# A mixture of 64 experts on one core: three sequences of the first layer are sorted by expert and run in units of 128 rows

## The chip, the core and the metric

The kernel runs on one NeuronCore of a Trainium2 chip. The metric is device time in microseconds for one execution. All arithmetic is float32.

## What is computed

The input `x` has 8 sequences of 512 tokens with 128 features. Three layers follow each other, each on a layer norm of the running sum: half of a mixture-of-experts block, a small mixing block along the sequence, and half of the same mixture-of-experts block again.

```python
def ffn(x):                      # xf: 4096 tokens x 128
    shared = silu(xf @ Ws_up) @ Ws_down            # 128 -> 64 -> 128
    aff = xf @ centroids.T                         # 64 experts
    _, idx = top_k(aff + expert_biases, 8)
    w = sigmoid(take_along_axis(aff, idx, axis=1))
    w = w / (sum(w, -1, keepdims=True) + 1e-8)
    cw = zeros((T, 64)).at[arange(T)[:, None], idx].add(w)
    h = silu(einsum('td,edf->etf', xf, W_up))      # 128 -> 64, every expert
    y = einsum('etf,efd->etd', h, W_down)          # 64 -> 128
    return shared + einsum('etd,te->td', y, cw)
x = x + 0.5 * ffn(layernorm(x))
x = x + mixing(layernorm(x))     # two 128x128 products, one gate per token
x = x + 0.5 * ffn(layernorm(x))
```

Each token uses 8 of the 64 experts; the weight of the other 56 in `cw` is zero. The reference computes all 64 and so does the kernel before.

## The kernel before, in words

An *item* is one sequence in one mixture-of-experts layer: 16 items, layer 0 first (`items`, L293). Within an item the experts go in 32 *pairs*. One step of the main loop (L478 on) is one pair of one item, 512 steps in all. In step n:

- `up(n)` (L419): one product of 128 x 128 weights (two experts side by side, `wup`) with 512 tokens (`ut`, tokens along the free side) into a bank of `ps_up`, then the silu on ScalarE into a tile `h` of the pool `hid`.
- `scale(n - SCALE_LAG)` (L428): VectorE multiplies `h` with the routing weights `cw` of the pair. These lie in SBUF repeated over the 64 rows of each expert. `load_cw` (L299) fetches them for GROUP pairs at a time, by two broadcasting transfers issued on SP, from `cw_t` in DRAM; after the last pair of a group has been scaled, `scale` calls `load_cw` for the group CW_BUFS further on.
- `down(n - DOWN_LAG)` (L437): one product of `wdn` with the scaled `h`, summed over all 32 pairs in a bank of `ps_y`. In between, the shared expert's product (L456) is added to the same bank.
- one step of `prep(i + 1)`, a generator: layer norm (`stats`, L181, with two small operations on GpSimd), turning, the shared expert's up and the affinities (L334), and the routing: eighth largest, weights, turned (`pc`, L387) and written to `cw_t`. In layer 1 the mixing block (`mix`, L219) comes first. Two steps after the last down of an item, `finish` adds the result to `x` (L409) and in layer 1 writes it out.

Every engine works its instructions in the order in which the program issues them: the schedule is written out by hand (`manual_schedule`). All DMAs are issued on SP. SCALE_LAG is 22, DOWN_LAG 25, GROUP 4, CW_BUFS 4. The start is set apart: the weights and two sequences are loaded ahead (L125 to L137); at step FIRST (14) of the first item its `prep` is run to its end, CW_BUFS groups are asked for, and then `load_rest` (L139) issues the rest of the down weights, the other six sequences and small constants, before any further group.

PSUM has eight banks: four for `ps_up`, two for `ps_y`, two for everything else (`ps_m`).

Of the kernel before, what the change touches and what calls it, by code (L numbers as in the profile page):

```python
# [8 lines left out]
F32 = mybir.dt.float32  # L9
AF = mybir.ActivationFunctionType  # L10
# [7 lines left out]
GROUP = 4  # L18
SCALE_LAG = 22
DOWN_LAG = 25  # L20
CW_BUFS = 4
FIRST = 14
SHARED = (8, 16)
# [3 lines left out]
def macaron_kernel(  # L27
# [33 lines left out]

    nc = tc.nc
# [5 lines left out]
    D1 = D + 1  # L68
    H = T // 2
# [9 lines left out]
    hid = ctx.enter_context(tc.tile_pool(name="hid", bufs=DOWN_LAG + 3))  # L79
    dram = ctx.enter_context(tc.tile_pool(name="dram", bufs=2, space=bass.MemoryType.DRAM))  # L80
    ps_up = ctx.enter_context(tc.tile_pool(name="ps_up", bufs=4, space=bass.MemoryType.PSUM))
    ps_y = ctx.enter_context(tc.tile_pool(name="ps_y", bufs=2, space=bass.MemoryType.PSUM))
    ps_m = ctx.enter_context(tc.tile_pool(name="ps_m", bufs=2, space=bass.MemoryType.PSUM))
# [17 lines left out]
    wup = const.tile([P, E, F], F32, name="wup")  # L101
    wdn = const.tile([P, NP, D], F32, name="wdn")
# [11 lines left out]
    def load_up(e0, e1):  # L114
        nc.sync.dma_start(
            out=wup[:, e0:e1, :], in_=w_up[e0:e1].rearrange("e d f -> d e f")
        )

# [20 lines left out]
    def load_rest():  # L139
# [4 lines left out]
        for s in range(2, B):  # L144
            load_x(s)
# [7 lines left out]
        nc.sync.dma_start(out=b_bc, in_=b.partition_broadcast(P))  # L153

    def transposed(dst, src, rows):
        ps = ps_m.tile([P, 512], F32, tag="m", name="turn_ps")
# [3 lines left out]
    turn_ps = ps_m.tile([P, 512], F32, tag="m", name="cent_ps")  # L160
# [8 lines left out]
    def make_mix():  # L169
        for k, (dst, src) in enumerate(((mix_b, wb_sb), (mix_bf, wbf_sb))):  # L170
            transposed(dst[:, :D], src, D)
            ps = ps_m.tile([P, 512], F32, tag="m", name="gate_ps")
# [5 lines left out]
        nc.scalar.mul(half_b, b_bc, 0.5)  # L178

# [17 lines left out]
    def normed(src, mv, rstd, width, name):  # L197
        u = norm.tile([P, NT, width], F32, tag=f"u{width}", name=f"u_{name}")
# [11 lines left out]
    def turned(dst, src, name, parts=1):  # L210

        for part in range(parts):
            js = range(part * NT // parts, (part + 1) * NT // parts)
            ps = ps_m.tile([P, len(js) * P], F32, tag="m", name=f"ps_{name}_{part}")
# [4 lines left out]
    def mix(s):  # L219
# [3 lines left out]
        u = normed(xt, mv, rstd, D1, f"mix{s}")  # L223

        for k, j in ((0, 0), (1, NT - 1)):
            ew = norm.tile([P, D], F32, tag="ew", name=f"ew{s}_{k}")
# [6 lines left out]
        ut = norm.tile([P, T + 1], F32, tag="mixt", name=f"mixt{s}")  # L233
# [5 lines left out]
        gam = small.tile([P, NT], F32, tag="gam", name=f"gam{s}")  # L239
        halves = []  # L240
        for half in range(NT // 2):
            pfb = ps_m.tile([P, 2, D1], F32, tag="m", name=f"pfb{s}_{half}")
            halves.append(pfb)
            for k in range(2):
# [20 lines left out]
            nc.scalar.activation(  # L265
                gam[:, 2 * half : 2 * half + 2],
                pfb[:, :, D],
                AF.Tanh,
                bias=half_b,
                scale=0.5,  # L270
            )
            yield
        sg = small.tile([P, NT], F32, tag="sg", name=f"sg{s}")
        nc.vector.tensor_scalar(sg, gam, 0.5, 0.5, ALU.mult, ALU.add)
        rest = small.tile([P, NT], F32, tag="rest", name=f"rest{s}")
        nc.vector.tensor_scalar(rest, gam, -0.5, 0.5, ALU.mult, ALU.add)
        for j in range(NT):
            nc.vector.scalar_tensor_tensor(
                xt[:, j, :],
                halves[j // 2][:, j % 2, :D],  # L280
                sg[:, j : j + 1],
                xt[:, j, :],
                ALU.mult,
                ALU.add,
            )
        yield
        for j in range(NT):
            nc.vector.scalar_tensor_tensor(
                xt[:, j, :], u[:, j, :D], rest[:, j : j + 1], xt[:, j, :], ALU.mult, ALU.add
            )  # L290
        yield

    items = [(layer, s) for layer in range(2) for s in range(B)]  # L293
    uts = {}
    shared = {}
    cw_ts = {}
    cw_tiles = {}

    def load_cw(g):  # L299

# [202 lines left out]
    for k in sorted(later):  # L503
        later[k]()
# [40 lines left out]
```

## Time and profile before

| what | value |
|---|---|
| median of 3 runs | 963.33 us (963.13 to 963.34) |
| the profiled execution itself | 963.14 us |
| its span, first to last instruction | 961.4 us |
| instructions | 8274 |
| TensorE clock granted | 1.000 |
| moved by DMA | 145.71 MB, mean 152 GB/s |

How to read it. The page gives the busy time of each engine (PE is TensorE, DVE is VectorE, ACT is ScalarE, POOL is GpSimd, SP the engine that issues the DMAs), the same in 40 slices of 24 us as tenths, the chain of work that ended last, and groups of instructions: line, engine, operation, output and inputs, shapes, count, then busy time and mean duration of one, and the idle time ahead of them with what ended it. A float32 product appears as two MATMUL instructions and two weight loads, a transpose as one. The ends of matmuls are modelled and overlap, so their cadence is read from the starts in the timeline.

### The profile page before, as it was taken

How to read it: one execution, taken by the hardware profiler on the slowest of the kernel's cores; microseconds unless marked ns; L12 is line 12 of the kernel's file. 1: busy time of each engine (PE TensorE's matmuls, PEld its weight loads, DVE VectorE, ACT ScalarE, POOL GpSimd, SP SyncE). 2: the span in 40 equal slices, each digit the busy share in tenths (PEclk: the TensorE clock that was granted, in tenths of full speed). 3: DMA queues.
4: the chain of work that ended last, by engine and by line, in shares of the span. 5: the costliest groups of instructions: out<-in, count | busy, mean ns of one | idle time of the engine just before them, and what ended most of it. 6: DMA issues, size and time to landing. Idle time of an engine off the chain costs nothing.

```text
span 961.4 us, 8274 instructions
## 1 busy us (share of the span) xinstructions
PE 949.5 (99%) x2535; PEld 441.6 (46%) x2535; DVE 476.0 (50%) x1282; ACT 398.6 (41%) x674; POOL 39.8 (4%) x73
## 2 busy tenths in 40 slices
PE   7999999999999999999999999999999999999998
PEld 3444444444444444454444544445444454444443
DVE  3453463515536253455464554645546455466243
ACT  6643353434434343344353443533435334353330
POOL 1000000000000000000000000000000000000000
PEclk9999999999999999999999999999999999999999
DMA  7999868496874869737677476784767848678933
GB/s 175 220 214 215 173 133 163 104 180 132 169 163 98 164 141 183 149 88 169 124 174 158 88 180 124 171 171 88 176 126 172 171 88 173 126 173 182 209 73 81
DMA packets 90188, 145.71 MB, mean 152 GB/s; under 512 B 10080, under 2 KB 24096, under 8 KB 90144
## 3 DMA queue, kind: packets, MB, share of 16 engines
q1 hardware_dynamic: 90144, 145.18, 71.9%
q8 instruction: 20, 0.33, 0.2%
q14 instruction: 24, 0.20, 0.1%
HBM read 140.97 MB, written 4.19 MB: 151 GB/s over the span
## 4 chain that ended last, share of the span: by engine, by line
PE 98%; ACT 1%; DVE 1%; DMA 0%; POOL 0%; issue 0%; ACTq 0%
PE y L441 46%; PE ph L423 45%; PE sl L334 2%; PE y L456 1%; PE po L407 1%; PE ps_ft L216 1%; PE pfb L253 1%; PE pfb L246 1%; PE pa L350 0%; PE ps_mixt L216 0%; PE pc L387 0%; ACT L425 0%; DMA x<-in_L_attn_u_dram 0%; ACT h L425 0%; DVE lg L343 0%; POOL rstd_f L194 0%
## 5 line engine op out<-in xcount | busy, mean ns | idle before, releaser
L423 PE MATMUL ph<-ut,wup 128*128 128x512 f32 x1024 | 522.7, 595 | 1.7 <-ACT h L425 1.7
L441 PE MATMUL y<-h,wdn 128*128 128x512 f32 x1024 | 519.0, 592 | 0.0
L425 ACT ACTIVATE h<-ph 128x512 f32<-128x512 f32 x512 | 303.3, 597 | 443.6 <-PE ph L423 414.6
L431 DVE TENSOR_TENSOR h<-h,cw 128x512 f32<-128x512 f32 x512 | 322.1, 682 | 51.7 <-DMA cw<-cw_t 49.2
L441 PEld LDWEIGHTS y<-h,wdn 128*128 128x128 f32 x1024 | 194.8, 190 | 244.6 <-issue 210.9
L423 PEld LDWEIGHTS ph<-ut,wup 128*128 128x128 f32 x1024 | 186.8, 191 | 196.0 <-issue 190.2
L409 DVE TENSOR_TENSOR x<-po,x 128x512 f32<-128x512 f32 (+1 forms) x17 | 11.2, 660 | 180.5 <-PE po L407 180.4
L343 DVE COPY lg<-sl 64x256 f32<-64x256 f32 x32 | 13.5, 422 | 99.5 <-PE sl L334 92.4
L262 DVE SCALAR_TENSOR_TENSOR pfb<-u_mix,ident,pfb 128x129 f32<-128x129 f32 x16 | 5.7, 356 | 93.8 <-PE pfb L253 80.1
L193 POOL TENSOR_SCALAR rstd_f<-mv_f 128x4 f32<-128x4 f32 (+1 forms) x17 | 8.7, 511 | 506.1 <-DVE mv_f L191 506.1
L200 DVE TENSOR_SCALAR u_f<-x,mv_f,rstd_f 128x128 f32<-128x128 f32 x64 | 17.9, 342 | 19.7 <-POOL rstd_f L194 19.7
L344 ACT ACTIVATE hsh<-sl 64x256 f32<-64x256 f32 x32 | 12.1, 378 | 32.6 <-DVE lg L343 32.6
L425 ACT ACT_TABLE_LOAD x16 | 20.5, 1283 | 0.3
L361 ACT ACT_TABLE_LOAD x16 | 20.5, 1283 | 0.3
L189 DVE BATCH_NORM_STATS2 st_f<-x 128x6 f32<-128x128 f32 x64 | 13.9, 277 | 12.7 <-DMA x<-in_L_attn_u_dram 12.7
L334 PE MATMUL sl<-ut,wsl 128*128 128x256 f32 x64 | 17.4, 397 | 0.0
L194 POOL TENSOR_TENSOR rstd_f<-rstd_f,minus_half 128x4 f32<-128x4 f32 (+1 forms) x17 | 16.8, 991 | 1.4
L193 POOL TENSOR_SCALAR rstd_mix<-mv_mix 128x4 f32<-128x4 f32 x8 | 4.6, 575 | 293.4 <-DVE mv_mix L191 293.4
L334 PEld LDWEIGHTS sl<-ut,wsl 128*128 128x128 f32 x64 | 12.4, 199 | 8.5 <-issue 6.7
L265 ACT ACTIVATE gam<-pfb,half_b 128x2 f32<-128x2 f32 x16 | 4.2, 262 | 25.2 <-DVE pfb L262 25.2
L325 ACT COPY ut<-ps_ft 128x512 f32<-128x512 f32 (+1 forms) x17 | 9.5, 560 | 12.2 <-PE ps_ft L216 12.2
L246 PEld LDWEIGHTS pfb<-mix_b,mixt 128*128 128x128 f32 x64 | 10.9, 191 | 7.6 <-issue 5.7
(69 smaller groups left out, 280.3 us busy)
## 6 DMA issues: line engine op xcount, KB each, us to landing
cw<-cw_t SPq DMA_DIRECT2D x256, 512.0 KB, 7.2
cw_t<-cw_sb SPq DMA_DIRECT2D x32, 64.0 KB, 4.2
x<-in_L_attn_u_dram SPq DMA_DIRECT2D x7, 256.0 KB, 5.7
out_dram<-x SPq DMA_DIRECT2D x7, 256.0 KB, 2.3
wdn<-in_L_ffn_W_down_dram SPq DMA_DIRECT2D x2, 512.0 KB, 5.9
wup<-in_L_ffn_W_up_dram SPq DMA_DIRECT2D x2, 256.0 KB, 4.2
wup<-in_L_ffn_W_up_dram SPq DMA_DIRECT2D x1, 512.0 KB, 6.9
x<-in_L_attn_u_dram SPq DMA_DIRECT2D x2, 128.0 KB, 2.2
```

Of the source, the lines that this page charges most:

```text
L189: nc.vector.bn_stats(st[:, j, :], src[:, j, :])
L193: nc.gpsimd.tensor_scalar(rstd[:, at], mv[:, at, 1], EPS_LN, None, ALU.add)
L194: nc.gpsimd.tensor_tensor(rstd[:, at], rstd[:, at], minus_half[:, at], ALU.pow)
L200: nc.vector.tensor_scalar(u[:, j, :D], src[:, j, :], mv[:, j, 0:1], rstd[:, j : j + 1], ALU.subtract, ALU.mult,)
L246: nc.tensor.matmul(pfb[:, k, :], lhsT=ut[:, j * P : (j + 1) * P], rhs=mix_b, start=True, stop=False,)
L334: nc.tensor.matmul(sl[:, k, :], lhsT=wsl[:, k, :, :].rearrange("d a f -> d (a f)"), rhs=ut[:, k * H : (k + 1) * H], start=True, stop=True,)
L343: nc.vector.tensor_copy(lg[other, :], sl[other, k, :])
L361: nc.scalar.activation(sig, pa, AF.Sigmoid)
L423: nc.tensor.matmul(ph, lhsT=w, rhs=uts[i], start=True, stop=True)
L425: nc.scalar.activation(h, ph, AF.Silu)
L431: nc.vector.tensor_tensor(h, h, cw_tiles[group][:, g, :], ALU.mult)
L441: nc.tensor.matmul(ys[i], lhsT=wdn[:, pair, :], rhs=hs.pop(n), start=pair == 0 and i % 2 == 0, stop=pair == NP - 1,)
```

## The change

Three of the eight sequences of layer 0 (5, 6 and 7) leave the dense stream, which keeps 13 items. They are handled beside it, in the same loop, by `background`, called once at the end of each step:

1. `sorted_chunk` prepares the three sequences one after the other (layer norm, turning, affinities, routing; the shared expert is added at once), then counts, by products with triangular matrices of ones, at which place of a list sorted by expert each token's eight copies lie, and in which place of a list in which each expert begins on a multiple of 128 rows.
2. For each tile of 128 tokens and each of its 8 experts, GpSimd scatters 128 rows of 512 B to `xsort` in DRAM: 96 indirect DMAs, at most POOL_RATE (1.25) per step.
3. 160 units of 128 rows, in quads of four, one quad every 3 steps: SP reads four row numbers into registers and loads the rows; ScalarE reads four expert numbers into registers and copies that expert's weights from `wup` and from `wtwice` (the down weights once more, in both halves of the partitions) to fixed places; TensorE turns the rows and runs up and down for one expert per unit; SP stores the result in `ysort` in DRAM.
4. GpSimd gathers, for each tile and each of its 8 experts, 128 rows of `ysort`: 96 indirect DMAs, again 1.25 per step; VectorE adds each, times its weight, to `x`, ADD_LAG (4) steps after its issue.

The lags of the dense stream become 9 and 11, its weights come in 3 groups of 2 pairs, FIRST is 8; `ps_up` has two banks, `ps_un` (transposes, units, results) two, and `ps_m` one for each of two streams. `load_rest` loads the sorted sequences first and gains `load_twice`.

The core of the diff:

```diff
-GROUP = 4
-SCALE_LAG = 22
-DOWN_LAG = 25
-CW_BUFS = 4
-FIRST = 14
-SHARED = (8, 16)
+GROUP = 2
+SCALE_LAG = 9
+DOWN_LAG = 11
+CW_BUFS = 3
+FIRST = 8
+SHARED = (16, 24)
+HID_BUFS = DOWN_LAG + 2
+CHUNKS = [(0, (5, 6, 7))]
+DENSE = [(0, s) for s in range(5)] + [(1, s) for s in range(8)]
+LATER_X = (5, 6, 7, 2, 3, 4)
+QUAD = 4
+UNIT_LAG = 4
+UNIT_PERIOD = 3
+POOL_RATE = 1.25
+BACK_BUFS = 7
+ADD_LAG = 4
...
-    hid = ctx.enter_context(tc.tile_pool(name="hid", bufs=DOWN_LAG + 3))
+    hid = ctx.enter_context(tc.tile_pool(name="hid", bufs=HID_BUFS))
+    unit = ctx.enter_context(tc.tile_pool(name="unit", bufs=2))
+    chunk = ctx.enter_context(tc.tile_pool(name="chunk", bufs=1))
+    back = ctx.enter_context(tc.tile_pool(name="back", bufs=BACK_BUFS))
     dram = ctx.enter_context(tc.tile_pool(name="dram", bufs=2, space=bass.MemoryType.DRAM))
-    ps_up = ctx.enter_context(tc.tile_pool(name="ps_up", bufs=4, space=bass.MemoryType.PSUM))
+    ps_up = ctx.enter_context(tc.tile_pool(name="ps_up", bufs=2, space=bass.MemoryType.PSUM))
     ps_y = ctx.enter_context(tc.tile_pool(name="ps_y", bufs=2, space=bass.MemoryType.PSUM))
-    ps_m = ctx.enter_context(tc.tile_pool(name="ps_m", bufs=2, space=bass.MemoryType.PSUM))
+    ps_m = ctx.enter_context(tc.tile_pool(name="ps_m", bufs=1, space=bass.MemoryType.PSUM))
+    ps_un = ctx.enter_context(tc.tile_pool(name="ps_un", bufs=2, space=bass.MemoryType.PSUM))
...
+    def load_twice(e0, e1):
+        for k in range(2):
+            nc.sync.dma_start(
+                out=wtwice[k * F : (k + 1) * F, e0:e1, :],
+                in_=w_down[e0:e1].rearrange("e f d -> f e d"),
+            )
...
-        for s in range(2, B):
+        for s in LATER_X:
             load_x(s)
...
+        for e in range(0, E, E // 4):
+            load_twice(e, e + E // 4)
...
+    def sorted_chunk(n):
+        layer, seqs = CHUNKS[n]
+        while not all(layer == 0 or (0, s) in finished for s in seqs):
+            yield
...
+        chosen = chunk.tile([P, G4, E], F32, tag="chosen", name=f"chosen{n}")
+        weight = chunk.tile([P, G4, E], F32, tag="weight", name=f"weight{n}")
+        sofar = chunk.tile([P, G4 + 1, E], F32, tag="sofar", name=f"sofar{n}")
+        us = []
+        nc.vector.tensor_scalar(sofar[:, 0, :], ones[:, :E], 0.0, None, ALU.mult)
+        for q, s in enumerate(seqs):
+            it = Item()
+            it.cw = weight[:, q * NT : (q + 1) * NT, :]
+            name = f"s{n}_{q}"
+            for _ in front(it, layer, s, name, keep=q):
+                yield
...
+            yield from routing(it, name, 0.5, "b", chosen[:, q * NT : (q + 1) * NT, :])
+            for r in range(q * NT, (q + 1) * NT):
+                nc.vector.tensor_tensor(
+                    sofar[:, r + 1, :], sofar[:, r, :], chosen[:, r, :], ALU.add
+                )
+            yield
+        cps = ps_un.tile([P, 512], F32, tag="un", name=f"cps{n}")
+        nc.tensor.matmul(cps[:E, :P], lhsT=sofar[:, g4, :], rhs=ones, start=True, stop=True)
+        crep = chunk.tile([E, P], F32, tag="crep", name=f"crep{n}")
+        nc.scalar.copy(crep, cps[:E, :P])
+        yield
...
+        ch.place = []
+        views = dram_disjoint_views(xsort, g4 * K)
+        strict = below[:E, :E].unsqueeze(1).to_broadcast([E, NT, E])
+        for q, s in enumerate(seqs):
+            at = slice(q * NT, (q + 1) * NT)
+            pos = ps_m.tile([P, 2, NT, E], F32, tag="b", name=f"pos{n}_{q}")
+            for k, lhsT in enumerate((crep, nrep)):
+                nc.tensor.matmul(
+                    pos[:, k, :, :], lhsT=below, rhs=chosen[:, at, :], start=True, stop=False
+                )
+                nc.tensor.matmul(
+                    pos[:, k, :, :], lhsT=ones, rhs=sofar[:, at, :], start=False, stop=False
+                )
+                nc.tensor.matmul(pos[:, k, :, :], lhsT=lhsT, rhs=strict, start=False, stop=True)
+            yield
...
+            share = chunk.tile([P, NT, K], F32, tag=f"share{q}", name=f"share{n}_{q}")
+            for r in range(NT):
+                for k in range(K):
+                    junk = small.tile([P, E], F32, tag="junk", name="junk", bufs=2)
+                    nc.vector.scalar_tensor_tensor(
+                        junk,
+                        key[:, 0, r, :],
+                        best[:, 0, r, k : k + 1],
+                        weight[:, q * NT + r, :],
+                        ALU.is_equal,
+                        ALU.mult,
+                        accum_out=share[:, r, k : k + 1],
+                    )
+                    if k % 4 == 3:
+                        yield
...
+                    pool_work.append(
+                        lambda u=us[q], place=place, r=r, k=k, v=views[
+                            (q * NT + r) * K + k
+                        ]: nc.gpsimd.indirect_dma_start(
+                            out=v,
+                            out_offset=bass.IndirectOffsetOnAxis(
+                                ap=place[:, 0, r, k : k + 1], axis=0
+                            ),
+                            in_=u[:, token_tile(r), :D],
+                            in_offset=None,
+                        )
+                    )
+        pool_work.append(lambda: coming_units.append(ch))
+    def load_unit(ch, g):
+        un = Item()
+        un.ch, un.g = ch, g
+        at = slice(QUAD * g, QUAD * (g + 1))
...
+        un.x = unit.tile([P, QUAD, D], F32, tag="ux", name=f"ux{ch.n}_{g}", bufs=3)
+        for k in range(QUAD):
+            nc.sync.dma_start(out=un.x[:, k, :], in_=ch.xsort[bass.ds(rows[k], P), :])
+        return un
+    def take(un, ks):
+        if ks[0] == 0:
+            at = slice(QUAD * un.g, QUAD * (un.g + 1))
+            _, un.experts = nc.values_load_multi_w_load_instructions(
+                un.ch.expert[0:1, at],
+                engines=[mybir.EngineType.Activation],
+                min_val=0,
+                max_val=E - 1,
+                skip_runtime_bounds_check_because="the experts are at most the last one here",
+            )
+            un.w = unit.tile([P, QUAD, DU], F32, tag="uw", name=f"uw{un.ch.n}_{un.g}")
+        for k in ks:
+            e = bass.ds(un.experts[k], 1)
+            at = slice(k % 2 * F, (k % 2 + 1) * F)
+            nc.scalar.copy(un.w[:, k, :F], wup[:, e, :].rearrange("p a f -> p (a f)"))
+            nc.scalar.copy(un.w[at, k, F:], wtwice[at, e, :].rearrange("p a f -> p (a f)"))
+    def turn_unit(un):
+        ps = ps_un.tile([P, QUAD, P], F32, tag="un", name="unx")
+        for k in range(QUAD):
+            nc.tensor.transpose(ps[:, k, :], un.x[:, k, :], ident)
+        un.xt = unit.tile([P, QUAD, P], F32, tag="uxt", name=f"uxt{un.ch.n}_{un.g}")
+        nc.scalar.copy(un.xt, ps)
+    def up_unit(un):
+        ps = ps_un.tile([P, QUAD // 2, P], F32, tag="un", name="unh")
+        for k in range(QUAD):
+            q, half = divmod(k, 2)
+            nc.tensor.matmul(
+                ps[half * F : (half + 1) * F, q, :],
+                lhsT=un.w[:, k, :F],
+                rhs=un.xt[:, k, :],
+                start=True,
+                stop=True,
+            )
+        un.h = unit.tile([P, QUAD // 2, P], F32, tag="uh", name=f"uh{un.ch.n}_{un.g}")
+        nc.scalar.activation(un.h, ps, AF.Silu)
+    def down_unit(un):
+        two = [ps_un.tile([P, QUAD // 2, D], F32, tag="un", name="uny") for _ in range(2)]
+        for k in range(QUAD):
+            q, half = divmod(k, 2)
+            rows = slice(half * F, (half + 1) * F)
+            nc.tensor.matmul(
+                two[half][:, q, :],
+                lhsT=un.h[rows, q, :],
+                rhs=un.w[rows, k, F:],
+                start=True,
+                stop=True,
+            )
+        un.y = unit.tile([P, QUAD // 2, 2, D], F32, tag="uy", name=f"uy{un.ch.n}_{un.g}")
+        nc.scalar.copy(un.y[:, :, 0, :], two[0])
+        nc.vector.tensor_copy(un.y[:, :, 1, :], two[1])
+    def store_unit(un):
+        dst = un.ch.ysort.rearrange("(u p) d -> p u d", p=P)
+        nc.sync.dma_start(
+            out=dst[:, QUAD * un.g : QUAD * (un.g + 1), :],
+            in_=un.y.rearrange("p q a d -> p (q a) d"),
+        )
+        un.ch.stored += 1
+        if un.ch.stored == un.ch.units // QUAD:
+            combine(un.ch)
...
+    def gather(ch, s, r, k, place, share):
+        t = back.tile([P, D], F32, tag="back", name="back")
+        nc.gpsimd.indirect_dma_start(
+            out=t,
+            out_offset=None,
+            in_=ch.ysort,
+            in_offset=bass.IndirectOffsetOnAxis(ap=place[:, 1, r, k : k + 1], axis=0),
+        )
+        def add():
+            j = token_tile(r)
+            nc.vector.scalar_tensor_tensor(
+                xs[s][:, j, :], t, share[:, r, k : k + 1], xs[s][:, j, :], ALU.mult, ALU.add
+            )
+            if k == K - 1 and r == NT - 1:
+                done(ch.layer, s)
+        sums.append((step + ADD_LAG, add))
...
+    def unit_stages(un):
+        return [
+            (UNIT_LAG, lambda: take(un, range(0, 2))),
+            (UNIT_LAG, lambda: turn_unit(un)),
+            (UNIT_LAG + 1, lambda: take(un, range(2, QUAD))),
+            (UNIT_LAG + 1, lambda: up_unit(un)),
+            (UNIT_LAG + 2, lambda: down_unit(un)),
+            (UNIT_LAG + 3, lambda: store_unit(un)),
+        ]
...
+    def background():
+        nonlocal credit, next_unit, current
+        if prepping[0] is not None and next(prepping[0], prepping) is prepping:
+            prepping[0] = None
+        while sums and sums[0][0] <= step:
+            sums.popleft()[1]()
+        running.sort(key=lambda x: (x[0], x[1]))
+        while running and running[0][0] <= step:
+            running.pop(0)[2]()
+        if current is None and coming_units:
+            current = coming_units.popleft()
+            current.g = current.stored = 0
+            next_unit = step + 1
+        if current is not None and step >= next_unit:
+            un = load_unit(current, current.g)
+            for at, what in unit_stages(un):
+                running.append((step + at, len(running) + 100 * step, what))
+            current.g += 1
+            if current.g == current.units // QUAD:
+                current = None
+            next_unit = step + UNIT_PERIOD
+        credit = min(credit + POOL_RATE, 4.0)
+        while pool_work and credit >= 1.0:
+            pool_work.popleft()()
+            credit -= 1.0
+    prepping = [None]
...
+                    prepping[0] = beside()
                 coming = prep(i + 1) if i + 1 < len(items) else None
+                if i + 1 < len(items):
+                    layer, s = items[i + 1]
+                    while layer == 1 and (0, s) not in finished:
+                        step += 1
+                        background()
...
-        if i == 2 and n < total:
+        if i == 1 and n < total:
             next(mixing, None)
+        background()
...
```

## The prediction, made before the changed kernel was run

> **What bounds the kernel now.** I read the page first: busy times, the 40 slices, the chain.
>
> ```profile
> PE 949.5 (99%) x2535; PEld 441.6 (46%) x2535; DVE 476.0 (50%) x1282; ACT 398.6 (41%) x674; POOL 39.8 (4%) x73
> PE   7999999999999999999999999999999999999998
> DMA  7999868496874869737677476784767848678933
> PE 98%; ACT 1%; DVE 1%; DMA 0%; POOL 0%; issue 0%; ACTq 0%
> L423 PE MATMUL ph<-ut,wup 128*128 128x512 f32 x1024 | 522.7, 595 | 1.7 <-ACT h L425 1.7
> L441 PE MATMUL y<-h,wdn 128*128 128x512 f32 x1024 | 519.0, 592 | 0.0
> L425 ACT ACTIVATE h<-ph 128x512 f32<-128x512 f32 x512 | 303.3, 597 | 443.6 <-PE ph L423 414.6
> L431 DVE TENSOR_TENSOR h<-h,cw 128x512 f32<-128x512 f32 x512 | 322.1, 682 | 51.7 <-DMA cw<-cw_t 49.2
> ```
>
> TensorE is full from slice 2 on and never waits for long; the chain is TensorE from end to end. DMA is the second resource: 72% on average, 9s at the start. The busy means overlap, so the true cadence comes from the timeline of TensorE in the steady part:
>
> ```profile
> 501.01 1.02 PE L423 MATMUL ph<-ut,wup 128*128 128x512 f32 x2
> 501.86 1.02 PE L441 MATMUL y<-h,wdn 128*128 128x512 f32 x2
> 502.72 1.02 PE L423 MATMUL ph<-ut,wup 128*128 128x512 f32 x2
> ```
>
> Start to start 0.859 us per product, 1.717 us per step (one up, one down). 512 steps are 879 us. From the same view: four transposes 0.44, L334 0.86, L456 0.63, L350 and L387 0.22 each, the mixing of a layer-1 item about 2.2. That is 2.8 per item, 5.0 in layer 1: 62 us. First up at 8.5 us, 4.8 after the last down, rest small waits: 961.4.
>
> Third view, SP's timeline in the first 60 us:
>
> ```profile
> 21.60 6.26 SPq L307 DMA_DIRECT2D cw<-cw_t  x8
> 27.91 2.38 SPq L142 DMA_DIRECT2D wsdn<-in_L_ffn_Ws_down_dram  x2
> 32.32 0.74 SPq L120 DMA_DIRECT2D wdn<-in_L_ffn_W_down_dram  x1
> 34.73 14.90 SPq L99 DMA_DIRECT2D x<-in_L_attn_u_dram  x6
> 54.26 1.28 SPq L307 DMA_DIRECT2D cw<-cw_t  x2
> ```
>
> Sixteen pairs' weights go out, then `load_rest`, and only at 54 us the next group. TensorE doesn't notice: it has 25 ups to do before its first down, and 16 pairs in hand.
>
> **What the Trainium skill says.** "DMA: Bandwidth & Descriptors", Queues, rings and completion order: an engine consumes descriptors in ring order. The trace agrees: all issues come from SP on one queue, and the group issued at 54.26 waits for everything ahead. "SBUF — State Buffer", two separate sides: VectorE with two SBUF inputs and a GpSimd op that reads SBUF exclude each other for a whole instruction. The trace agrees: L193 takes 0.23 us at 18.92 with VectorE idle, but 0.58 at 51.02, where it ends 0.1 after the L431 that began at 50.85. "ScalarE: Activation LUTs", What ACT_TABLE_LOAD costs: 186 ns + 0.833 ns per element, neighbours overlapping by 93 ns. For 512 that is 613; L425 shows 597. "DMA: Bandwidth & Descriptors", Latency and other measured facts: about 1 us for GpSimd to emit a DMA, and a 600 ns floor for a register load; nothing before shows either.
>
> **The change, part by part** (against the profiled span of 961.4; the profiled execution took 963.14, 1.7 more, and the median of the runs is 963.33).
>
> *Dense work removed.* 3 items x 32 steps x 1.717 = -164.8. Their `po` and `pc` go: 3 x 0.66 = -2.0. Turning, L334, L350 and the shared product stay, in sorted form.
>
> *TensorE work added.* 3 x 512 x 8 / 128 + 64 = 160 units, always run, in 40 quads. Per quad: four transposes 0.44; up, 4 products of 128 columns x 2 instructions, 8 x 0.11 (pfb's cadence: eight in 0.89) = 0.88; down likewise, but on alternating halves of the rows, where L456 ran at 0.63 instead of 0.86, so 0.63. Together 1.95; x 40 = +78. Positions: per sequence 6 products of 256 columns at 0.43, x 3 = +7.7; counts about +1. TensorE's sum: -80, to 881.
>
> *The start.* CW_BUFS 3 x GROUP 2 = 6 pairs are loaded ahead instead of 16, and the first down comes after 11 ups instead of 25. `load_rest`, queued on SP between group 2 and group 3, gains `wtwice`: 64 x 64 x 128 x 4 B x 2 = 4.2 MB. Timing it: cw_t(0) lands near 23 (21.5 before, plus 1.7 because two `ps_up` banks hold TensorE back behind the routing's table loads). Then 1.57 MB of cw at 210 GB/s (the rate of the full slices) to 31; wdn 1.05 MB to 35.5; six x of 0.26 MB at 290 GB/s to 41; small ones 3 us (49.67 to 53.4 before) to 44; wtwice, 64 partitions per transfer like cw, at 215 GB/s 19.5 us to 64; group 3 lands at 66. Ahead of down(6) TensorE has only 18 ups and 6 downs (20.6) and 4.3 of preparation: done at 33.5. It stands 32.5 us, where before it stood 2. So **+30**; 25 if wtwice moves at 290 GB/s, 37 at 160. In that stall VectorE also sits in front of `bn_stats` on x5, hidden under the same wait.
>
> *Units on ScalarE.* TensorE's in-order stream makes `up_unit` wait for ScalarE. Per quad, from the end of up(n): TensorE does down 0.86, turn 0.44, up 0.86, down 0.86, two of four up products 0.44: at 3.45 it wants the third unit's weights. ScalarE in the same time: silu 0.60 (the sequencer fetches four registers meanwhile), register load, four copies, `xt` copy 0.56, silu(n+1) 0.60, four copies. A copy of 64 elements is 0.22 to 0.26 (L163: 215 ns; 203 ns for one element from SBUF), one of 128 is 0.27 to 0.31, overlap 0.1: 0.7 per four, and I take 0.9 for the register addresses. Register load: 0.6 (floor above) to 2.4 (four such in a row); I take 1.3 (the price that "Runtime: NRT & Kernel Launch", The ~15µs preamble/postamble breakdown, gives for a few registers in one go). So 1.4 + 0.9 + 0.56 + 0.6 + 0.9 + 0.1 = 4.5: TensorE stands about **1.1 us per quad, +44**. Ends: 0.1 (+4) and 3.1 (+124). Below nothing isn't possible: the copies shorten nothing. `ps_up` of two banks alone hides a table load pair plus sigmoid (2.95 us): up(n+3) wants its bank 3.7 after silu(n) begins.
>
> *SP, in units.* Per quad 6 cw issues at 0.55, four unit loads at 0.6, a store 0.5, a register load 1.3: 7.6 us, in a quad of 3 x 1.717 + 1.95 + 1.1 = 8.2. Just covered. Behind a blocked SP issue stand the cw loads, and behind those VectorE's scaling and the downs; six pairs, some 10 us, are the cover. DMA per quad: 0.79 MB cw in 3.8 us plus 0.52 MB in about 2.3: covered.
>
> *Pool.* 96 scatters, 96 gathers, issued at 1.25 per step, so Pool may take 1.37 us each (1.45 with the preparation in the steps). Price: 1.0 to emit, plus a share of the lock against L431 (0.68 of 1.72 us busy): I take 1.2, hidden. Ends 0.6 and 2.0. Queued behind them on Pool are `rstd` of every dense item, and for gathers the sums on VectorE; so a slow Pool slows everything. DMA there: 0.26 MB cw in 1.25 us plus 80 KB in 0.4 per step, 1.65 of 1.72: barely.
>
> *VectorE.* 96 share operations, four per step, 0.25 each (L365, 64 wide: 0.21), with scaling 0.63: about a step; where dense preparation falls in, 0.7 more. Scaling now runs 2 steps ahead of its down (9 against 11; before 3). I put down **+15** for Pool, VectorE, SP and single PSUM buffers together: 5 for VectorE's overlap, 5 for the last scatter's landing ahead of the first unit loads, 5 for `ps_un`. Ends 0 and +100.
>
> *Sum:* 881 + 30 + 44 + 15 = 970, + 1.7 = 972.
>
> **Rivals.**
> *Faster: the units are cheap.* If ScalarE's dynamic copies overlap as static ones do and the register load hides under the silu (0.4 us stall per quad, +16) and the rest costs 8, it is 881 + 30 + 16 + 8 + 1.7 = 937. For it: ScalarE is 41% busy. Against: the wait is one of order, not of load. The point of decision: 881 + 30 + 1.7 leaves 50.6 us; with my 15 beside it, ScalarE's stall turns the sign at 35.6 / 40 = 0.9 us per quad.
> *Pool is the bound.* At 2.0 us per indirect DMA 192 take 384 us, against 154 steps x 1.85 = 285: 972 + 99, less 11 of the 15: 1060. For it: the lock of L193 and nothing indirect in the trace. Against: the 1 us of the page.
> *The loads of the start stay hidden* (SP gets group 3 out early): 972 - 28 = 944. Against: program order puts 7 MB in front of it.
>
> **How the numbers follow.** Forecast, slower through start and units, 961 to 1020: 0.49, of which 0.04 lies within 0.2%. Cheap units: 0.34. Pool: 0.11. Start hidden: 0.06. Both signs have weight: the forecast's own range is 961 to 1020, and the range to hold 8 in 10 runs from 925 (0.2 us per quad, 5 for the rest: 881 + 30 + 8 + 5 + 1.7) to 1040 (Pool at 1.8 us). Faster by over 0.2%: cheap units, start hidden, 0.40 in all; within 0.2% (what a measurement of this kernel can tell from no change) 0.04; slower 0.56.
>
> **What would show it.** L423 and L441 x832 each. In the slices, TensorE low in slices 2 and 3, with a wait for cw of over 10 us on VectorE and the issue of wtwice on SP ahead of it; if TensorE is full there, the start is wrong. In the middle third, waits of the `unh` products for ScalarE of about 1 us, 40 times; near 0 makes the kernel faster. On Pool, mean spacing of scatters under 1.4 us; above that, `rstd` waits and VectorE's waits for `back` appear. A quad in 8.2 us; if SP's issues fill it, SP is the bound that I called covered.

## The result and the profile after

The changed kernel took 1084.51 us (1081.02 to 1088.44, 4 runs) beside 963.34 (963.13 to 963.41) for the kernel before on the same chip: ratio 1.126, 95% interval 1.121 to 1.131. The profiled execution took 1088.44 us, its span 1086.7. The same kernel later took 982.7 us on one chip and 1090.4 on another, while the kernel before took 963.1 to 963.8 on all of them. So there are two questions: where do 19 us come from on every chip that it met, and where another 100 on some?

The page of the changed kernel, first set: busy times; the slices of 27 us for TensorE, GpSimd and TensorE's clock; the chain; the four dense groups.

```profile
PE 940.6 (87%) x2989; PEld 444.2 (41%) x2989; DVE 502.8 (46%) x1591; ACT 460.1 (42%) x1011; POOL 241.5 (22%) x272
...
PE   6529999529958999998998999899869779999998
...
POOL 2000023740671300000000000004762764110000
PEclk9669999859978999999999999999979979999999
...
PE 76%; issue 8%; ACT 5%; another core or an unknown queue 4%; SPq 3%; DMA 2%; DVE 1%; POOL 1%; ACTq 0%; POOLq 0%; DVEq 0%
...
L792 PE MATMUL ph<-ut,wup 128*128 128x512 f32 x832 | 455.7, 632 | 80.6 <-issue 50.0
L810 PE MATMUL y<-h,wdn 128*128 128x512 f32 x832 | 438.1, 611 | 30.8 <-DVE h L800 30.8
L794 ACT ACTIVATE h<-ph 128x512 f32<-128x512 f32 x416 | 247.4, 597 | 425.5 <-PE ph L792 280.9
L800 DVE TENSOR_TENSOR h<-h,cw 128x512 f32<-128x512 f32 x416 | 274.1, 683 | 92.8 <-DMA cw<-cw_t 74.3
```

Read the holes in the PE row. The first, slices 1 to 3, was forecast. Those of slices 8, 9 and 12, and the shallower ones of slices 30, 32 and 33, were not; all lie under GpSimd's busy slices, and L792's 50 us of "issue" is time in which TensorE stood for nothing that the profile names.

The start, from SP's timeline, then VectorE's waits in the first 110 us:

```profile
23.29 3.90 SPq L362 DMA_DIRECT2D cw<-cw_t  x6
...
29.71 7.78 SPq L123 DMA_DIRECT2D x<-in_L_attn_u_dram  x6
...
42.12 19.07 SPq L147 DMA_DIRECT2D wtwice<-in_L_ffn_W_down_dram  x8
61.29 3.09 SPq L522 DMA_DIRECT2D xsort<-zeros  x1
64.48 12.58 SPq L362 DMA_DIRECT2D cw<-cw_t  x8
```

```profile
DVE h L800 <- DMA cw<-cw_t: 20.4, 1, 20.4
DVE st_fs L256 <- DMA x<-in_L_attn_u_dram: 19.2, 1, 19.2
```

Group 3 is asked for at 64.5 us, behind wtwice, as forecast, and VectorE waits 20.4 us for it. Ahead of that it stands 19.2 us in front of x5.

The unforecast hole, from the timeline of all engines around slice 8 (start, duration, engine, line, then the idle time before and what ended it):

```profile
218.85 1.92 PE L810 MATMUL y<-h,wdn 128*128 128x512 f32 x2
...
232.26 0.96 POOL L657 DMA_INDIRECT xsort<-u_fs,place  x1 [0.30 <-issue]
233.53 0.96 POOL L657 DMA_INDIRECT xsort<-u_fs,place  x1 [0.30 <-issue]
240.19 0.76 DVE L625 SCALAR_TENSOR_TENSOR key<-pos,chosen 128x256 f32<-128x256 f32 x2 [12.86 <-remote]
240.24 1.09 ACT L794 ACTIVATE h<-ph 128x512 f32<-128x512 f32 x2 [23.30 <-remote]
...
240.88 2.08 PE L792 MATMUL ph<-ut,wup 128*128 128x512 f32 x2 [20.12 <-ACT h L794]
```

TensorE's last product ends at 220.8. ScalarE's next silu, though the product that it takes had ended, starts only at 240.24. VectorE, ScalarE and TensorE come back within 0.7 us of each other, 6 us after the last of a run of 40 scatters, which GpSimd issued at an undisturbed 1.26 us each. I call this a *stop*. Between 220.8 and 240 VectorE made two small operations and the other two none.

### The profile page after: what moved, and what is told of

The parts are those of the page before. It is cut to its first block, busy times and chain, and to the rows that moved or that the text cites. A ratio compares the mean times of both kernels' runs of the same rounds, so it can differ in the third digit from the quotient of the medians.

```text
span 1086.7 us, 11559 instructions
## 1 busy us (share of the span) xinstructions
PE 940.6 (87%) x2989; PEld 444.2 (41%) x2989; DVE 502.8 (46%) x1591; ACT 460.1 (42%) x1011; POOL 241.5 (22%) x272
## 4 chain that ended last, share of the span: by engine, by line
PE 76%; issue 8%; ACT 5%; another core or an unknown queue 4%; SPq 3%; DMA 2%; DVE 1%; POOL 1%; ACTq 0%; POOLq 0%; DVEq 0%
PE ph L792 33%; PE y L810 30%; PE unh L714 3%; PE uny L729 2%; SPq L147 2%; PE unx L706 1%; ACT h L794 1%; PE sl L393 1%; POOL back L766 1%; ACT L794 1%; PE y L826 1%; DMA x<-in_L_attn_u_dram 1%; ACT L425 1%; DMA cw<-cw_t 1%
## 5 line engine op out<-in xcount | busy, mean ns | idle before, releaser
L792 PE MATMUL ph<-ut,wup 128*128 128x512 f32 x832 | 455.7, 632 | 80.6 <-issue 50.0
L810 PE MATMUL y<-h,wdn 128*128 128x512 f32 x832 | 438.1, 611 | 30.8 <-DVE h L800 30.8
L794 ACT ACTIVATE h<-ph 128x512 f32<-128x512 f32 x416 | 247.4, 597 | 425.5 <-PE ph L792 280.9
L800 DVE TENSOR_TENSOR h<-h,cw 128x512 f32<-128x512 f32 x416 | 274.1, 683 | 92.8 <-DMA cw<-cw_t 74.3
L810 PEld LDWEIGHTS y<-h,wdn 128*128 128x128 f32 x832 | 163.5, 197 | 240.6 <-issue 179.0
L792 PEld LDWEIGHTS ph<-ut,wup 128*128 128x128 f32 x832 | 146.1, 197 | 221.5 <-issue 167.9
L766 POOL DMA_INDIRECT back<-ysort,place x96 | 103.3, 1076 | 77.5 <-issue 36.7
L657 POOL DMA_INDIRECT xsort<-u_fs,place x96 | 98.0, 1021 | 72.7 <-DVE junk L640 44.3
L714 PE MATMUL unh<-uxt,uw 128*64 128x128 f32 x320 | 42.1, 296 | 18.0 <-ACT uw L700 13.6
L701 ACT COPY uw<-wtwice 64x128 f32 x160 | 47.0, 294 | 1.5
L714 PEld LDWEIGHTS unh<-uxt,uw 128*64 128x64 f32 x320 | 23.5, 136 | 52.2 <-ACT uxt L708 25.6
L700 ACT COPY uw<-wup 128x64 f32 x160 | 38.7, 242 | 2.1 <-issue 0.6
L775 DVE SCALAR_TENSOR_TENSOR x<-back,share,x 128x128 f32<-128x128 f32 x96 | 32.9, 346 | 14.1 <-DMA back<-ysort,place 9.6
L737 ACT COPY uy<-uny 128x256 f32<-128x256 f32 x40 | 14.9, 372 | 34.5 <-PE uny L729 33.7
```

The source lines that it names most:

```text
L657: ]: nc.gpsimd.indirect_dma_start(
L700: nc.scalar.copy(un.w[:, k, :F], wup[:, e, :].rearrange("p a f -> p (a f)"))
L701: nc.scalar.copy(un.w[at, k, F:], wtwice[at, e, :].rearrange("p a f -> p (a f)"))
L714: nc.tensor.matmul(ps[half * F : (half + 1) * F, q, :], lhsT=un.w[:, k, :F], rhs=un.xt[:, k, :], start=True, stop=True,)
L766: nc.gpsimd.indirect_dma_start(out=t, out_offset=None, in_=ch.ysort, in_offset=bass.IndirectOffsetOnAxis(ap=place[:, 1, r, k : k + 1], axi ...
L775: nc.vector.scalar_tensor_tensor(xs[s][:, j, :], t, share[:, r, k : k + 1], xs[s][:, j, :], ALU.mult, ALU.add)
```

## Experiments

The runs were made in sets, each on one chip, so each run is compared with one on its own chip. Where an experiment leaves out the scatters, the units read rows of the input x instead. Two stretches of the main loop show stops directly: steps 64 to 128 (scatters) and 272 to 336 (gathers), from the starts of L792's products.

| kernel | chip | time, us | steps 0-32 | 64-128 | 144-256 | 272-336 |
|---|---|---|---|---|---|---|
| changed, first set | not recorded | 1084.5 | 97.7 | 186.1 | 324.6 | 160.2 |
| a2: changed | 6 | 982.7 | 99.4 | 119.5 | 323.2 | 120.9 |
| a3: changed | 1 | 1090.4 | 101.0 | 190.7 | 323.4 | 158.9 |
| e1: no scatters, no gathers | 6 | 980.8 | 98.8 | 119.5 | 323.3 | 120.9 |
| e2: no scatters | 6 | 982.5 | 100.1 | 119.5 | 324.0 | 120.9 |
| e3: paced scatters | 6 | 984.7 | 98.7 | 119.5 | 324.2 | 121.1 |
| e3b: the same | 1 | 1056.4 | 99.2 | 162.9 | 324.1 | 147.8 |
| e4: late wtwice | 6 | 962.1 | 79.3 | 119.5 | 325.9 | 120.9 |
| e5: copied row numbers | 6 | 990.0 | 100.2 | 124.8 | 325.9 | 121.4 |
| e6: start spread | 6 | 948.9 | 65.7 | 119.5 | 323.2 | 120.9 |
| e6b: the same | 4 | 951.6 | 68.9 | 119.5 | 326.0 | 120.9 |
| e8: x5 early | 6 | 983.5 | 98.6 | 119.5 | 324.3 | 121.7 |
| e9: scatters twice | 1 | 1195.5 | 99.5 | 290.9 | 323.4 | 156.6 |
| e10: no weight copies | 1 | 1053.7 | 100.1 | 187.0 | 291.1 | 159.5 |
| e11: units only moved | 1 | 989.0 | 100.4 | 187.9 | 229.6 | 147.1 |
| e12: plain Pool DMAs | 1 | 1020.7 | 100.0 | 119.5 | 323.2 | 157.0 |
| e13: Pool sums | 1 | 1014.8 | 99.1 | 119.5 | 325.7 | 148.3 |
| e14: rests | 4 | 1008.3 | 98.3 | 128.0 | 324.9 | 120.9 |
| e14b: the same | 15 | 1006.7 | 99.3 | 126.7 | 323.2 | 120.9 |

**My first theory and its rivals.** Theory 1: DMAs that GpSimd (Pool) issues one after the other without a pause hold the other engines up. Rival 2: it is the transfers themselves. Rival 3: it is Pool being busy. Rival 4: the time is lost in the start and in the units, with their engines. Below, a *run* of DMAs is a row of them in which none starts more than 2.0 us after the one before.

*e1 and e2.* In place of the scatter, `pool_work.append(lambda: None)`; e1 drops the gather and its sum too.

> Leaves out: the 96 scatters and the 96 gathers with their sums; the units read 128 consecutive rows of the input x in place of xsort. TensorE, ScalarE, the SP loads and stores of the units and the places of all steps stay. Theory 1 (software DMAs issued by Pool without a pause hold up what the other engines tell each other): 1084 - 70 (scatters) - 42 (gathers) - 5 (96 sums on VectorE) = 967, between 950 and 985. Rival 4 (the loss sits in the start and in the units, with VectorE, ScalarE and SP): 1060 to 1080. Between 1000 and 1040 both would hold in part.

> Leaves out the 96 scatters alone (the units read rows of the input x; gathers and sums stay). Theory 1: 1084 - 70 = 1014 (1000 to 1030), and the gaps in 200 to 250 and 300 to 350 us of the trace are gone while those of the gathers, 30 to 45 us, stay. Rival 4: over 1060.

They took 980.75 and 982.53 us, where 967 and 1014 were expected. Against 1084 this looked like theory 1, but e2 keeps its gathers in runs of up to 28 and shows no stop, which theory 1 doesn't allow.

*e3.* `nc.vector.tensor_copy(at, place[:, 0, r, k : k + 1])` ahead of each scatter, which then takes its rows from `at`.

> Same work; each scatter takes its row numbers from a small copy that VectorE makes in the scatter's own step, so Pool can't run ahead of the steps. Bytes, number of DMAs and steps are as in the changed kernel. Theory 1 (it is the run without a pause): 1020 (1005 to 1045), about what leaving the scatters out gives. Rival 2 (the transfers themselves, by their writes to DRAM or their share of the queues): 1075 to 1095. Rival 3 (Pool's issue beside VectorE's work, paced or not): 1075 to 1095.

It took 984.67 us, 35 below the expectation, for a reason that e3 didn't contain: the chip, as a2 and a3 will show.

*e4.* `load_twice` is taken out of `load_rest` and issued in eight parts, in steps 44, 52, ... 100:

```diff
+        if n in twice_at:
+            load_twice(twice_at[n], twice_at[n] + E // 8)
```

> The four pairs of loads of wtwice (4.2 MB written) leave the start: eight pairs, one each at steps 44, 52, ... 100, all ahead of the first unit. Forecast's step: the 30 to 40 us that TensorE stands in the first 100 us are the wait for the weights of the third group of pairs behind these loads: 1084 - 30 = 1054 (1045 to 1065). Rival: a start that ends earlier only lets the scatters meet the same stop earlier, or the x rows set the start: 1075 to 1090.

It took 962.14 us (20 runs; ratio to before 0.9987, 0.9980 to 0.9994), 92 below the expectation, with a run of 40 scatters in it and no stop. A shorter start can't have removed 122 us. Three results in a row far below what I expected, all on chip 6, pointed at the comparison itself; so the next set had the changed kernel itself in it.

*a2, e5, e8, e6.* e5: row numbers copied at once for a whole sequence. e8: `load_x(LATER_X[0])` ahead of `load_rest`. e6: e4 and e8, with the rest of `load_rest` issued one load per step.

> The changed kernel itself once more, beside the others. If the stops of 183 to 240 and 283 to 335 us belong to the kernel: 1075 to 1095 again, with the same gaps. If they belonged to the chip or to that one set of runs: 980 to 990, what the version with paced scatters took, since its start is still the slow one.

> Control for the paced version: the scatters take their row numbers from a copy too, but VectorE makes it at once for a whole sequence, so nothing ties a scatter to its step. Pacing is the remedy: 1075 to 1095 as the changed kernel. Any small shift of the program is: 980 to 990.

> One line moved: x of sequence 5 is loaded ahead of the first weights of groups, in a stretch in which SP is idle, in place of behind half of w_down. VectorE's wait of 19 us at the head of the first sorted front goes; the wait for the weights of the third group, behind the loads of wtwice, stays. If the two waits are one behind the other: -19 against the changed kernel without its stops (985), so 966; if the second wait only grows by what the first one loses: 980 to 985. With the stops of Pool's bursts still in: 85 to 100 more.

> Both repairs of the start: x of sequence 5 early, the loads of wtwice in steps 44 to 100, and the other loads of the start one per step from step 10. Against the version with late wtwice alone (962): the first 16 steps took 46 us there and 16 in the kernel before; with the wait for x gone, 962 - 20 = 942 (935 to 950). If another load is late next: 955 to 962.

a2: 982.70 us (ratio 1.020, 1.018 to 1.022), with runs of 40 and 38 scatters, as in the first set. The page of a2:

```profile
PE   6428999999999899989998999899999999999998
...
L810 PE MATMUL y<-h,wdn 128*128 128x512 f32 x832 | 427.2, 597 | 32.9 <-DVE h L800 32.9
L792 PE MATMUL ph<-ut,wup 128*128 128x512 f32 x832 | 439.4, 612 | 3.9 <-ACT h L794 3.9
```

Only the hole of the start is left; the 50 us of "issue" are gone. The same 20 us of a trace, first set, then a2 (PE, PEld, DVE, ACT, POOL busy; clock; DMA share; GB/s):

```profile
220.00:240.00 20.00, 0.77 (x1) 0.00 (x0) 0.85 (x2) 0.00 (x0) 11.14 (x12) 0.50 0.12 39
```

```profile
220.00:240.00 20.00, 20.00 (x50) 8.76 (x49) 12.29 (x38) 6.86 (x12) 14.42 (x15) 1.00 0.94 252
```

The program is the same to the instruction, and Pool issues at nearly the same pace in both (the first 40 scatters take 51.2 and 53.2 us). Length of the run alone is thus no cause on chip 6: theory 1, as I stated it, falls, and so does what I had read from e3 and e4. Against a2, e1 and e2 say that scatters cost 0 and gathers 2 us on chip 6, and e4 that late wtwice is worth 20.6 us. e5 took 990.0, 7 more than a2; 5 of them in steps 64 to 128; what a copy of row numbers moves there I didn't follow.

e8 took 983.54 us. The wait only moved: VectorE's wait for cw grew from 22.1 us (a2) to 31.5.

```profile
DVE h L801 <- DMA cw<-cw_t: 37.0, 2, 31.5
```

e4 had the mirror image, 20.3 us in front of x5 with cw in time:

```profile
DVE st_fs L253 <- DMA x<-in_L_attn_u_dram: 20.3, 1, 20.3
```

Two loads are late one behind the other in one in-order queue. e6 mends both: 948.86 us, 33.8 below a2, 0.986 of before (0.983 to 0.989).

*a3, e9, e10, e11.* e9: each scatter is issued a second time, into a tensor that nobody reads. e10: no copies of weights and no register loads on ScalarE; all units take the weights of experts 0 to 3. e11: the units are only loaded and stored.

> The changed kernel unchanged, once more: 981 to 985 if the second set is the rule; 1080 to 1090 if the stops come back.

> Every scatter is made twice, the second time into a tensor that nobody reads: 192 software DMAs in front of the units in place of 96, in runs of up to 80 without a pause. If the stops of the first set come from the number of software DMAs in a row, they show here: 60 us or more over the 983 of the changed kernel. If Pool's DMAs hide as long as Pool keeps up: Pool then needs 96 x 1.26 = 121 us more before the units may start, and the units come that much later beside the dense steps, with nothing on TensorE's path: 983 to 995.

> Leaves out ScalarE's copies of each unit's weights and its register loads; every unit takes the weights of experts 0 to 3. TensorE, VectorE, SP and Pool as in the changed kernel. Forecast's step: TensorE waits 1.1 us per quad for ScalarE, 40 x 1.1 = 44, so 983 - 44 = 939. Rival: the waits of the products for uw and uxt in the trace are 18 us in all, and uxt stays: 983 - 14 = 969. If VectorE or SP are late next in the units: 975 to 983.

> Leaves out the work of the units on TensorE, ScalarE and VectorE (turn, up, silu, down, copies); SP still loads each quad and stores it, Pool scatters and gathers. Forecast's steps: units cost TensorE 78 and the wait for ScalarE 44: 983 - 122 = 861. If SP's or Pool's part of the units were what costs: 920 to 983.

This set ran on chip 1. a3: 1090.44, the stops back in the same steps. Against a2, scatters lose 71.2 us and gathers 38.0; together 109, the whole difference (107.7). e9 takes 105 us more than a3, and the loss in steps 64 to 128 goes from 71 to 171. A window of 60 us of e9, most of it in the second half of a run of 80 scatters that ends at 294 us:

```profile
240.00:300.00 60.00, 15.94 (x22) 5.32 (x22) 8.01 (x37) 2.99 (x5) 40.96 (x43) 0.59 0.22 65
```

So on this chip the loss grows with the scatters, faster than their number; e9 makes the runs longer too and doesn't part the two. e10 takes 36.7 less than a3 (its runs lie 11 us apart), where the forecast's step was 44; in the steps 128 to 256, where nothing stops, 34.5 less. The wait itself, a2 and then e10:

```profile
L714 PE MATMUL unh<-uxt,uw 128*64 128x128 f32 x320 | 41.9, 294 | 18.0 <-ACT uw L700 13.6 <-ACT uxt L708 4.3
```

```profile
L700 PE MATMUL unh<-uxt,wup 128*64 128x128 f32 x320 | 26.3, 285 | 0.0
```

18.0 us idle, and 15.6 more inside the products' busy time: the idle column alone shows about half of such a wait. e11 is no clean measure: 101 below a3 instead of the forecast's 122 (78 for the products, 44 for the wait), because another wait comes up. In its steps 144 to 256 VectorE waits 93.6 us for cw, behind unit loads on SP that wait 32.4 us for earlier stores.

*e3b, e12, e13*, on chip 1 again. e12: `nc.gpsimd.dma_start` to fixed rows in place of the scatter; e13: `nc.gpsimd.tensor_tensor(spare, ones[:, :NT], minus_half, ALU.pow)`.

> The version with paced scatters once more, for a chip on which the changed kernel stops (1090). There the steps 272 to 336, beside the gathers, which are not paced, take 85 to 100 us in place of 57, which shows that it is such a chip. Pauses are what matters: steps 64 to 80 take 33 us and the whole about 1090 - 68 = 1022. Number of software DMAs or anything else: 72 and 1080 to 1095. On a chip that doesn't stop: 985, as before.

> The 96 scatters become plain DMAs that Pool issues to 128 consecutive rows each (the rows of xsort are then not sorted, and the units compute on unsorted rows). Number, bytes and queue are the same, only the row numbers are gone. If any DMA issued by Pool's software does it: as the changed kernel on the same chip (1090, or 983 on one that doesn't stop). If the form with row numbers does it: 1090 - 68 = 1022 on a chip that stops.

> Leaves out the scatters; in the place of each, Pool computes a power of 128 x 4 numbers, 1.0 us long (the units read rows of the input x). If Pool need only be busy, in a row, for the others to stop: as the changed kernel on the same chip. If it takes its DMAs: 1022 on a chip that stops, 983 on one that doesn't.

In all three the others stop beside the gathers (steps 272 to 336, in the order e3b, e12, e13: 147.8, 157.0 and 148.3), so it is such a chip. Steps 64 to 128 take 119.5 us in e12 and e13, as on chip 6: no stop. Pool's row of what stands for the scatters, e12 first with TensorE in a window of 60 us, then e13 (from 150 to 400 us):

```profile
L657 POOL DMA_DIRECT2D xsort<-u_fs x96 | 51.7, 546 | 1.7 <-DMA xsort<-u_fs 1.5
...
180.00:240.00 60.00, 60.00 (x158) 27.84 (x157) 45.90 (x222) 23.81 (x39) 23.43 (x44) 1.00 0.77 201
```

```profile
L656 POOL TENSOR_TENSOR spare<-ones,minus_half 128x4 f32<-128x4 f32 x87 | 99.9, 1148 | 6.5
```

Forty plain DMAs 0.53 us apart stop nobody, nor do Pool's computations of 1.15 us. So number and bytes of the transfers (rival 2) and a busy Pool (rival 3) are not enough; what the stops need is the form with row numbers. Whether it is the issue of that form (a run of 40 lasts 51 us with it, 22 without) or its writes to scattered rows, e12 doesn't part. Pacing (e3b) only helps: 1056 where I had expected 1022 if pauses are what matters, 43 us lost in steps 64 to 128 in place of 71, since the paced scatters still came in runs of up to 27.

*e14, e14b, e6b.* e14: three of e13's operations after every eighth scatter.

> After every eighth scatter Pool computes three powers of 1.0 us each, so no nine scatters follow each other without a rest. On a chip that stops (the steps 272 to 336 beside the gathers take over 80 us): if the unbroken run counts, steps 64 to 128 take 120 to 130 us as on chip 6 (190 in the changed kernel on chip 1), and the whole about 1090 - 68 + 20 for units that start later = 1042 (1020 to 1055). If the number of scatters counts, rests or not: 180 or more, and 1090 to 1120. On a chip that doesn't stop: 983 to 1005.

> The version with the repaired start (949 on chip 6) once more. On a chip that stops: if the stops are independent of the start, 1090 - 34 = 1056 (1045 to 1065); if they need the late start, as the 962 of the late wtwice on chip 6 first suggested, 949 to 960. On one that doesn't stop: 949.

> The version with rests once more. On a chip that stops (steps 272 to 336 over 80 us): steps 64 to 128 take 129 us as on chip 4 if the unbroken run counts, and 180 or more if the number of scatters does; the whole 1040 to 1055 or 1090 to 1120. On one that doesn't stop: 1008.

They ran on chips 4 and 15, neither of which stops: 1008.26 and 1006.73 (rests cost some 25 us), and for e6 again 951.61 (0.987, 0.981 to 0.994).

**Open.** Why chip 1 (two sets) and the first set stop, and 4, 6 and 15 don't; whether rests keep the stops away; what e6 takes on a chip that stops. If stops are independent of the start, 949 + 109 = 1058, an estimate from a3 and a2, and slower than before. Set against the same steps of a2, a run of 40 scatters that lasts 51 us loses 38 (first set, a3), one of 27 in 37 us 20 (e3b), one of 80 in 102 us 88 (e9), and the run of nine that comes first (first set, a3) nothing. So a run under some ten may go free; that is read, not tried.

**A rival that no run tests: the recording.** The traces come from a profiler in the hardware, which writes a record of every event while the kernel runs. In a trace, the landing of a DMA leaves 16 updates of a semaphore: 5216 for the 326 DMAs of the kernel before, and all 11024 are there in e1. With row-number DMAs on chips 4, 6 and 15 an execution lacks 33 to 104 of 12,560 to 14,224. On chip 1 and in the first set it lacks 1673 (e13) to 5141 (e9), in the first set 3537 of 14096, and they are missing where the stops are. In a3, 1704 of 3328 are there in steps 48 to 144, 4854 of 4944 in steps 144 to 256, and 1395 of 3248 in steps 256 to 350; in e12, with plain DMAs in place of the scatters, none is missing in steps 48 to 144. So where the engines stop, the trace loses records. Every time above comes with a span and a clock read from the same execution, so each of them was recorded, and no execution without recording is on record. The stops may cost a kernel that nobody records the same, less, or nothing. What is shown is what row-number DMAs do in recorded executions on such a chip.

## Why the prediction was wrong, step by step

The ends of matmuls are modelled and overlap, so TensorE's work is counted here from start to start, less idle time.

| step | forecast | measured | from |
|---|---|---|---|
| dense steps, po, pc | -166.8 | x832 each, as said | page |
| units' products | +78 | 70 | e10: up 23.5, down 28.9, turn 17.5 |
| changes of the array's shape beside them | not named | 16 | below |
| positions, counts | +8.7 | 11 | a2 |
| start | +30 | 34 | a2 less e6 |
| TensorE waits for ScalarE | +44 | 35 | a3 less e10 in steps 128 to 256 |
| Pool, VectorE, SP, PSUM | +15 | 21, of which 2 for scatters, gathers, sums | what is left of a2; a2 less e1 |
| sum, with 963.3 | 972 | 983 | a2: 982.7 |
| stops | not named | 102 to 109 | first set, a3 |

**Right, on a chip that doesn't stop.** Start, units and the sign held, and 982.7 lies in the forecast's own range. VectorE's wait for cw is there at 20 us, with wtwice ahead of it on SP. But "hidden under the same wait" of x5 was half the truth: it is hidden only while the other stays (e4, e8). A quad: steps 160 to 256 of a2 are 32 quads in 279.4 us, 8.73 each; less 15 us of preparation of three layer-1 items by the forecast's 5.0, 8.26 against 8.2. That the sum comes within 11 us is in part luck: the units' products and the waits for ScalarE were put 18 too high, and the other rows 28 too low.

Not named: what TensorE loses when the shape that the profile prints (`128*128`, `128*64`, `64*128`) changes from one product to the next. A quad in a2:

```profile
451.89 1.02 PE L810 MATMUL y<-h,wdn 128*128 128x512 f32 x2
452.75 0.60 PE L706 MATMUL unx<-ident,ux 128*128 128x128 f32 x4
453.19 1.02 PE L792 MATMUL ph<-ut,wup 128*128 128x512 f32 x2
454.05 1.02 PE L810 MATMUL y<-h,wdn 128*128 128x512 f32 x2
455.00 0.93 PE L714 MATMUL unh<-uxt,uw 128*64 128x128 f32 x8
455.86 1.12 PE L792 MATMUL ph<-ut,wup 128*128 128x512 f32 x2
456.82 1.02 PE L810 MATMUL y<-h,wdn 128*128 128x512 f32 x2
457.78 0.72 PE L729 MATMUL uny<-uw,uh 64*128 64x128 f32 x8
458.42 1.13 PE L792 MATMUL ph<-ut,wup 128*128 128x512 f32 x2
```

From L810 to the transposes, which have its shape, 0.86 us go by, as between two dense products. From L810 to `unh` or `uny`, and from the L792 behind these to the next L810, 0.95 to 0.96. Over the whole stretch the median is 94 ns on the way in and 104 on the way out, and it is the same in the kernel before on both sides of the shared product (`64*128`, 16 times). Two ways in and two out per quad are 0.4 us, 16 for 40 quads: an estimate from these medians. The transposes are short too and cost nothing extra, so it isn't the shortness. No run changes the shapes alone.

**Wrong: the Pool step.** The forecast priced an indirect DMA at 1.2 us, found a break-even at 1.37 and called it hidden. The price holds: 0.96 us and 0.30 to the next. The cover holds too on chip 6: VectorE stands 20.0 us in all for gathered rows (a2, L775), but steps 272 to 336 take 120.9 us with gathers and without (a2, e1). What failed is the assumption behind "hidden", that an engine off the path costs others only by being late or by the lock against VectorE. On chip 1 and in the first set a run of row-number DMAs stopped TensorE, ScalarE and VectorE alike while Pool kept its pace: in the first set 67 us more than a2 in steps 64 to 128 (186.1 against 119.5) and 39 in steps 272 to 336 (160.2 against 120.9), where the step had nothing. Why they stop, and whether they would without recording, stays open. The rival "Pool is the bound" (1060) was near in number and is not what happened: Pool was done early, and in a stop it works undisturbed. The +100 end of the +15 had the size, but as Pool's slowness, with a chance of 0.11; the trace of before, with nothing indirect in it, could not show the mechanism, and the range had no place for it.

## What to carry to other kernels

Before an experiment is compared with a kernel, run that kernel on the same chip: three of my first four expectations missed by 31 to 92 us because their base came from a set with stops and they ran on a chip without. When all engines come back at the same moment, look for the one that never stopped, and give its work another form before blaming traffic or load; then count the records of the trace, and ask whether the recording takes part. In an in-order queue, mend all late loads together; one alone may gain nothing (e8: nothing; e4: 21 us; both, with the rest spread: 34).

## What the runs showed of the hardware that I had not expected

- Indirect DMAs of 128 rows, issued back to back by GpSimd 1.26 us apart: harmless on three chips; on chip 1 and in the first set, in recorded executions, TensorE, ScalarE and VectorE all but stand and SP issues little until some 6 us after the run (0.77 us of TensorE in 20), and about half of the records of landings are missing there. Plain DMAs on the same engine, 0.53 us apart, do neither.
- A change of the array's shape between neighbouring products costs TensorE 94 ns on the way to the smaller one and 104 on the way back (a2, e6, e10; 64 rows in before too).
- A plain DMA on GpSimd takes 0.54 us of the engine, one with row numbers 0.96 us and 0.30 to the next.
- In and after a stop TensorE's granted clock is lower (first set: 0.71, 0.50 and 0.85 in the 20 us windows from 200 to 260; a2: 1.00 in all three).
